# A vision tower whose instruction orders come from a planner: other durations in the planner, token requests as a queue of their own, and another written order for TensorE

## The chip, the core and the metric

The kernel runs on one core of a Trainium2 chip. A core has a matrix engine (TensorE, PE in the profile; its weight loads stand apart as PEld), three engines for element-wise work (VectorE or DVE, ScalarE or ACT, GpSimd or POOL) and SyncE (SP), which here issues DMA requests. Each engine takes its own instructions in their order and waits on semaphores for the others. The metric is the device time of one execution in microseconds (us); lower is better.

## What is computed

One tokenizer and one transformer layer over 16 images of 3 x 512 x 512, each cut into 1,024 patches of 16 x 16, with 256 features and 8 heads of 32. All in float32:

```python
h = patches(x) @ tok_W.T + tok_b                      # 16 x 1024 x 256
a = layernorm(h)
q, k, v = split(a @ w_qkv)                            # 8 heads of 32
k = sum(kan_a[f] * sin((f + 1) * k) + kan_b[f] * cos((f + 1) * k) for f in range(256))
h = h + softmax(q @ k.T * 32**-0.5) @ v @ w_out + b_out
a = layernorm(h)
shared = mlp(a, sW1, sW2, sW3)                        # 256 -> 256 -> 128 -> 256, relu
gate = softmax(a @ gW)                                # 4 experts, the best two kept
h = h + shared + sum(softmax(best two of gate) * expert(a))   # 256 -> 128 -> 64 -> 256
```

The sums over 256 frequencies for each of the keys' 16 x 1024 x 256 elements are the heavy part outside the matrix products.

## The kernel before

**The pieces.** An image's keys are worked through in 32 *groups* of 8 rows. A group needs three wave tiles of 128 x 1024. The two slow ones (`w`) are loaded by DMA, broadcast from the keys' angles in DRAM (`ud`, `load_waves`). The fast one (`f`) is spread by VectorE's shuffle from a tile `src` (`load_source`, `spread_waves`). GpSimd multiplies each tile by its lane's integer frequency (`turn_waves`, `L1026`), ScalarE takes its sine (`sine`, `L1036`). Then TensorE mixes the two slow tiles with the coefficients (`mix`, `L1056`, output `kan`), VectorE multiplies by the fast one (`times_fast`, `L1070`), and TensorE adds the products of two groups up (`add_up`, `L1089`, output `red`). Eight groups make the keys of a pair of heads; they go through DRAM (`kd`) into `k4`. An *attention* (half the queries of one pair, 8 an image, 128 in all) has 8 scores (`score`, `L1155`, output `sT`), 8 exponentials (`exponential`, `L1170`, `es`) and 8 weighings of the values (`weigh`, `L1188`, `av`), followed on VectorE by a reciprocal, two products and a check (`normalize`).

**Rounds.** Four groups and one attention make a round. ScalarE's big work has a fixed order: a round's twelve sines (six for each two groups), a load of the exponential's table, and eight exponentials of the attention two rounds behind; the next round's first sine loads the sine's table again.

**The chains.** All the rest (tokens, layernorms, keys, queries, values, projection, gates, networks) is written as Python generators on four chains, which `yield` the engine that they need and a duration. `tokens` is on chain 3, with first layernorms; keys, queries and values on chain 0; projection, gates and networks on chain 1. Their TensorE pieces share two PSUM banks, `side0` and `side1`. `kan` and `sT` tiles share two others in turn, so each waits until the tile two before it has been used up: a `kan` by `L1070`, an `sT` by its exponential.

**The planner.** `run` goes through a written order, `ORDER`: one character for each of TensorE's 3,840 pieces (M mix, R add_up, S score, W weigh, a digit for the next piece of that chain). Before each it lets the other engines do whatever they can start up to TensorE's own time (`others`), each the step that can start first by the planner's clocks. Each step has a cost and the steps that it depends on (`put`), and when a step is laid, its instructions are recorded on its engine in that order. On the chip only the orders remain, with semaphores between them: the clocks decide the order on VectorE, ScalarE's chain work, GpSimd and SyncE, and nothing else.

`ORDER` has a head of 664 pieces, a block of 240 pieces (one image's worth) eleven times, and a tail of 536.

**Tilings.** `mix` uses the array as 64 x 32 tiles, `av`, `red`, `gate` and the experts' second layer as 128 x 32, scores and transposes whole. A chain piece of the kind `ANY` takes the tiling that the array is in, by `tiling_of`; as 128 x 32 it issues four narrow matmuls (`L322`) for each whole one (`L319`). `retile` puts a cost on a change of tiling.

**Token requests.** There are three `x` buffers. `tokens` multiplies a chunk of 128 patches, calls `load_x` for the chunk three ahead, which waits for the same buffer, and then has VectorE add the bias:

```python
            del chunks[b, j]
            load_x(b, j + XBUFS)
            for action in deferred.pop(j + b * (N // XT), ()):
                action()
            yield DVE, 0.41
            nc.vector.tensor_add(h[:, t, :], ps, tokb)
```

`transfer` keeps SyncE's clock and that of the DMA engines; `sent` is the same for a store that a chain makes.

Of the kernel before, what the change touches and what calls it, by code (L numbers as in the profile page):

```python
# [22 lines left out]
N = 1024  # L23
# [20 lines left out]
XT = 128  # L44
# [13 lines left out]
LAG, LANDS, TABLE, PER_COLUMN = 0.06, 2.0, 1.28, 1.0 / 600  # L58
SWITCH = {None: 0.21, (128, 32): 0.13, (64, 32): 0.13}
# [6 lines left out]
    "333333313131300003000030M0M000MMR3R3M3M",  # L66
    "303RMM3MR330M3R3M03MSSRSSWSSWSSWWWW0MWM",
    "WMMRSSSRSWSSWSSW0WWWWMMW3MMRSSRSSWSSWSSW0WW0MMWWWMMRSSRSSWSSWSSW0WWMWWMWMRMSSSWSSWSSWSRW"
    "WWWWMMMMRSSSWSSWSSWSRWWWWW0M0MM0RMS0SSWSSWSWSWSWWW3W3MR13M3MMRSSRSSWSS1SSWWWW3WMWWM3RMS1"
    "SS1SS0SSWWWMS3WR3WWWWM0MMRMS0SS1SR1SSWW1S1SW0W1WW1MMW1W1MM1SSRWSS0SS1WSSWW10RWMWWW1MM10M"  # L70
    "S1SSRWSWR1SS1WSS1W1MMWWMMWW0SS1R1SS1WW1SS1SSW1WRW1WMMW3WMMRS1SS1SW1SS3SSW1WR1WWWWWMM13MM"
    "1RSS0SS0SS0SWWWSWWWR3MMW1WS10S1RSS1S3MMWSS3WRWWSW1WWMW31MM0SS1SSRMS1SSWWWSWR3WWWW3MM131M"
    "S1RSSWWMWSSR3S1S3S1WWW01M1WW1MM0RSS1SWSSWMS1SSWRWW01MW1WWMM101SSRMW1SSWWSS1RSS101MMWWWWW"
    "MS3SSWRMWSS1S01SSW1RW0W3MMWWRWSS131SS1MMWWSS1SSRWWW1WWW101",
    (
        "MM10RMM1SS01SS1SS1WWSS1WWWRWWWMM10MMRS3S1SS1SSWWWSS3RWWWW1W3MM0RMM3SSRSWWWSS1SS1S3WWWMMW"
        "3W311MSRM1WS1S3SWWS3S1SSRW1W0WMM1WWRMM10SS1SS1WW1SS0SSWWRW1WWW0MM10MM1SS1RRWWSS0S1SWSS1W"
        "WWWWMM1S0SRWSSWMMWS1S31SSWRW3WW1WMM3MMR1SS1SS1SSWWWSS1WRWW1WW101"
    )
    * 11,  # L80
    "MM1MM1SSRRWWS1S0SS0SSWWW130MMWW1WRM1MS1",
    "3SSRWWWSS31SS1SW1WWWWMM3RM1S0SSWSS1SSWWMSWR3WWM3WWMM13S1SR1MSWWRS3S1SWS3SWWW01MM1WW10MMR"
    "1SS1SSRWSS1S1WWS0WWWWWMM101MM1SS1RS1SRSSWWWSS01WWMMWWWMS1SSWSSRW0SS1S1WMWWR1WWMM10W1MMR1"
    "SS1SSWWSS1SSWWWR1WM1WW101MM10S1MR1SSWRS1SWSSWS1WWMMWWWRMM1SS0SSWWSSWSSRWWW1WW1M0M1RSS1SS"
    "WSSWSMWSM1WWRWM1W1WMM1RM1SS1SSWWSS1SSWR1W1W1W1MM1WWR1SM1SS1SSWWSSWS1MWWRWMWWM1SS1SWSMSRM"
    "WS1SS1WR1WWW1WW1MM1M1RSS1SWWSS1SSWSWMWW1RW1MM1RW1MM1SSR1SSWWSS1WWSSWWWW1SSSWSSWWSSWSSWWW"
    "W1SS1SS1SWWSSWWWWWW11110110111110000101000100101001000100",
# [3 lines left out]
def plain_path(ctx: ExitStack, tc: tile.TileContext, a: dict, out: bass.AP, verdict: bass.AP):  # L91
# [185 lines left out]
    locks = set()  # L277

# [10 lines left out]
    def retile(tiling):  # L289

        same = now["tiling"] == tiling
        now["tiling"] = tiling
        return 0.0 if same else SWITCH[tiling]

# [35 lines left out]
    def transfer(took, issue=0.0, ready=0.0):  # L330

        clock[SP] = max(clock[SP], ready) + issue
        now["dma"] = max(now["dma"], clock[SP]) + took
        return now["dma"] + LANDS

    def sent(took, issue):

        return transfer(took, issue, chains[now["chain"]]["ready"])
# [9 lines left out]
    def step(c):  # L348

        ch = chains[c]  # L350
        now["chain"] = c
        bank, ch["bank"] = ch["bank"], None
        need = ch["need"]
        before = now["stream"]
        on = need[0] if isinstance(need, tuple) and need[0] in clock else None
        if on == PE:
            now["piece"] = tiling_of(need[2])
        if on:
            at = max(clock[on], ch["ready"] + LAG)
            if on == PE:  # L360
                at = max(at, banks(c)[0][0] + LAG)
            ch["ready"] = clock[on] = at + (need[1] or 0.0)
            if bank is not None:
                free[bank] = ch["ready"]
        elif isinstance(need, tuple):
            ch["ready"] = max(ch["ready"], done[need])
        while True:
            if ch["gen"] is None:
                if not ch["gens"]:
                    ch["need"] = None  # L370
                    break
                ch["gen"] = ch["gens"].pop(0)
            try:
                ch["need"] = next(ch["gen"])
                break
            except StopIteration:
                ch["gen"] = None
        if on == PE:
            took = PER_COLUMN * (now["stream"] - before) + retile(now["piece"])
            now["piece"] = None  # L380
            ch["ready"] = clock[PE] = at + took
# [31 lines left out]
    def lay(engine, queue):  # L413
# [3 lines left out]
        done[key] = clock[engine]  # L417
# [37 lines left out]
    def lay_fixed(kind):  # L455

        cost, deps, key, action = queues[PE][kind][0]
        user = USERS.get(kind)
        at = begin(PE, deps + (bigs[-2:-1] if user else []))

        def lay_it():
            queues[PE][kind].pop(0)
            clock[PE] = done[key] = at + cost + retile(TILINGS.get(KINDS[kind]))
            if user:
                bigs.append((user, *key[1:]))
            action()

        return at, lay_it
# [27 lines left out]
    def load_x(b, j):  # L496

        b, j = b + j // (N // XT), j % (N // XT)
        if b < B:
# [5 lines left out]
            done["x", b, j] = transfer(1.75, 0.6, clock[PE])  # L505
# [38 lines left out]
    def tokens(b, half):  # L544
# [5 lines left out]
        for t in range(4):  # L550
# [13 lines left out]
            load_x(b, j + XBUFS)  # L564
            for action in deferred.pop(j + b * (N // XT), ()):
                action()
            yield DVE, 0.41
            nc.vector.tensor_add(h[:, t, :], ps, tokb)  # L568
# [94 lines left out]
    def values(b):  # L663
# [5 lines left out]
        for t0 in range(0, NT, 2):  # L669
# [11 lines left out]
            yield ACT, 0.62  # L681
# [142 lines left out]
    def networks(b, half, late=False):  # L824
# [25 lines left out]
        def first_of_expert(e):  # L850
            yield ANY
            ps = hidden(lambda c: w1e[:, 2 * e + c, :], "e1p")
            yield ACT, 0.6
# [4 lines left out]
        def second_of_experts(u, e1):  # L858
# [11 lines left out]
            yield ACT, 0.6  # L870
# [15 lines left out]
        for m in range(2):  # L886
            yield ANY
            ps = hidden(lambda c, m=m: w1s[:, c, ts(m, P)], "s1p")
            yield ACT, 0.6
# [14 lines left out]
        yield ACT, 0.6  # L904
# [42 lines left out]
        done["written", b, half] = sent(1.6, 0.5)  # L947
# [13 lines left out]

    def load_waves(g, j):


        def action():
# [6 lines left out]
            done["loaded", g, j] = transfer(1.9)  # L972
# [3 lines left out]
        put(SP, "waves", 1.1, deps, ("load", g, j), action)  # L976

    def load_source(p):


        def part(j, blk):
            def action():
# [11 lines left out]
                landed = transfer(0.4)  # L994
# [7 lines left out]
        for j in range(2):  # L1002
            for blk in range(2):
                put(SP, "source", 1.4, deps, ("part", p, j, blk), part(j, blk))

    def spread_waves(g):
# [11 lines left out]
        put(DVE, "spread", 1.28, deps, ("spread", g), action)  # L1018

    def turn_waves(g, j):  # L1020
# [8 lines left out]
        put(POOL, "turn", 1.87, [dep], ("turn", g, j), action)  # L1029

    def sine(g, j, change):
# [8 lines left out]
        put(ACT, "fixed", 0.96 + change, [("turn", g, j)], ("sine", g, j), action)  # L1040
# [26 lines left out]
    def times_fast(g):  # L1067
# [4 lines left out]
        put(DVE, "prod", 1.16, [("mix", g), ("sine", g, 2)], ("prod", g), action)  # L1072
# [29 lines left out]
    def finish_keys(p):  # L1102


        def action():
# [3 lines left out]
            done["kd", p] = transfer(1.4, 1.1, done["keys", p])  # L1109
# [4 lines left out]
    def stack_keys(p, half):  # L1114

        def action():
# [3 lines left out]
            done["stacked", p, half] = transfer(1.9)  # L1120

        deps = [("kd", p)] + ([("score", 2 * p - 1, 4 * half + 3)] if p > 0 else [])
        put(SP, "keys", 0.8, deps, ("k4", p, half), action)
# [3 lines left out]
    def stack_queries(att):  # L1127
# [3 lines left out]
        def action():  # L1131
# [8 lines left out]
            done["q4", att] = transfer(1.6)  # L1140

        deps = [("queries", b, i // 2)] + ([("score", att - 2, NT - 1)] if att > 1 else [])
        put(SP, "queries", 2.0, deps, ("q", att), action)
# [6 lines left out]
    def score(att, kc):  # L1150
# [13 lines left out]
        put(PE, "S", 0.47, deps, ("score", att, kc), action)  # L1164

    def exponential(att, kc):
# [9 lines left out]
        put(ACT, "fixed", 0.99, deps, ("exp", att, kc), action)  # L1176
# [28 lines left out]
    def normalize(att):  # L1205
# [8 lines left out]
        def divide(half):  # L1214
# [11 lines left out]
            put(DVE, "norm", 0.4, deps, ("divide", att, half), action)  # L1226
# [15 lines left out]
        put(DVE, "norm", 1.67, [("av", att, NT - 1)], ("reciprocal", att), reciprocal)  # L1242
        for half in range(2):
            divide(half)
        put(DVE, "norm", 0.4, [("divide", att, 1)], ("norm", att), check)
# [30 lines left out]
    for g in range(total):  # L1276
# [6 lines left out]
        times_fast(g)  # L1283
    for p in range(total // 8):
# [7 lines left out]
    for rd in range(B * RI + 2):  # L1292
# [15 lines left out]
        put(ACT, "fixed", TABLE + 0.2, [], ("table", rd), table)  # L1308
# [752 lines left out]
```

## Time and profile before

| | us |
|---|---|
| median of 3 runs (3911.86 to 3915.78) | 3914.31 |
| the profiled execution | 3913.84 |
| its span, first to last instruction | 3912.3 |
| TensorE's mean granted clock | 0.994 of full |

The longest groups (busy time, mean duration in ns, idle time of the engine just before them and what ended most of it):

```profile
L1026 POOL TENSOR_TENSOR w<-w,lane 128x1024 int32<-128x1024 int32 x1024 | 1925.6, 1897 | 391.6 <-DMA w<-ud 273.0
L1170 ACT ACTIVATE es<-sT 128x1024 f32<-128x1024 f32 x1024 | 1014.9, 1022 | 340.9 <-PE sT L1155 296.8
L1036 ACT ACTIVATE w<-w 128x1024 f32<-128x1024 int32 x1024 | 1013.3, 1046 | 70.5 <-POOL w L1026 67.3
...
L1155 PE MATMUL sT<-q,k 128*128 128x512 f32 x2048 | 708.1, 455 | 22.0 <-ACT es L1170 12.3
L1011 DVE STREAM_SHUFFLE f<-src 128x1024 int32<-128x1024 int32 x512 | 683.1, 1373 | 0.4
L1188 PE MATMUL av<-es,v 128*32 128x256 f32 x8192 | 638.7, 383 | 14.8 <-ACT es L1170 12.3
```

A matmul of float32 operands stands in the trace as two records, one of the scores' and of `wb` as one; overlapping records of TensorE are normal, since matmuls are pipelined and a record's end is modelled.

### The profile page before, as it was taken

The numbers are of one execution on the slowest core, as the hardware profiler recorded it, in microseconds if no ns is written. First come the engines' busy times: TensorE is split into PE (matmuls) and PEld (weight loads), VectorE is DVE, ScalarE is ACT, GpSimd is POOL, SyncE is SP. The second block draws the span as 40 slices with busy tenths as digits, with TensorE's granted clock in tenths as the row PEclk, the third lists the DMA queues.
The fourth block names the chain that finished last, engine by engine and source line by source line (L and its number), as shares of the span: only waits on it lengthen the run. The fifth ranks groups of instructions, "written<-read, shape, count | busy, mean of one in ns | idle before, by whom it ended". The sixth has DMA issues, their size and how long they took to land.

```text
span 3912.3 us, 102935 instructions
## 1 busy us (share of the span) xinstructions
PE 3811.7 (97%) x40337; PEld 1949.1 (50%) x40337; DVE 2525.4 (65%) x4075; ACT 3264.3 (83%) x3939; POOL 3197.1 (82%) x2328
## 2 busy tenths in 40 slices
PE   7899999999999999999999999999999999999998
PEld 4334454554545555455454545545455554544444
DVE  4756757666675766757667575766767667576552
ACT  2788888888888888888888888888888888888983
POOL 3988879788788878879788788878879888888870
PEclk9999999999999999999999999999999999999999
DMA  7997968888788888878888788787878888778760
GB/s 231 283 255 213 278 197 248 256 230 259 214 260 231 233 262 228 259 218 257 243 236 260 211 255 249 225 255 222 267 214 252 258 226 265 223 231 254 213 179 21
DMA packets 589665, 916.53 MB, mean 234 GB/s; under 512 B 60877, under 2 KB 179573, under 8 KB 589173
## 3 DMA queue, kind: packets, MB, share of 16 engines
q1 hardware_dynamic: 588036, 909.40, 80.0%
q8 instruction: 321, 5.26, 0.6%
q14 instruction: 172, 1.40, 0.1%
q10 hardware_dynamic: 1136, 0.47, 0.0%
HBM read 758.64 MB, written 150.99 MB: 233 GB/s over the span
## 4 chain that ended last, share of the span: by engine, by line
PE 70%; ACT 9%; DMA 9%; POOL 4%; DVE 3%; issue 3%; SPq 1%; ACTq 0%; POOLq 0%; DVEq 0%
PE av L1188 17%; PE sT L1155 10%; PE kan L1056 9%; DMA w<-ud 6%; PE red L1089 4%; PE tok L319 4%; ACT w L1036 3%; PE e1p L319 3%; PE e3p L319 3%; PE tok L322 3%; POOL w L1026 2%; ACT f L1036 2%; PE e1p L322 2%; ACT es L1170 2%; PE s1p L319 2%
## 5 line engine op out<-in xcount | busy, mean ns | idle before, releaser
L1026 POOL TENSOR_TENSOR w<-w,lane 128x1024 int32<-128x1024 int32 x1024 | 1925.6, 1897 | 391.6 <-DMA w<-ud 273.0
L1170 ACT ACTIVATE es<-sT 128x1024 f32<-128x1024 f32 x1024 | 1014.9, 1022 | 340.9 <-PE sT L1155 296.8
L1036 ACT ACTIVATE w<-w 128x1024 f32<-128x1024 int32 x1024 | 1013.3, 1046 | 70.5 <-POOL w L1026 67.3
L1026 POOL TENSOR_TENSOR f<-f,lane 128x1024 int32<-128x1024 int32 x512 | 971.4, 1897 | 105.2 <-DVE f L1011 89.8
L1070 DVE TENSOR_TENSOR f<-kan,f 128x1024 f32<-128x1024 f32 x512 | 605.0, 1214 | 207.9 <-ACT f L1036 112.1
L1155 PE MATMUL sT<-q,k 128*128 128x512 f32 x2048 | 708.1, 455 | 22.0 <-ACT es L1170 12.3
L1011 DVE STREAM_SHUFFLE f<-src 128x1024 int32<-128x1024 int32 x512 | 683.1, 1373 | 0.4
L1188 PE MATMUL av<-es,v 128*32 128x256 f32 x8192 | 638.7, 383 | 14.8 <-ACT es L1170 12.3
L1188 PE MATMUL av<-es,ones 128*32 128x256 f32 x8192 | 631.0, 380 | 0.0
L1056 PE MATMUL kan<-w,coef 64*32 64x512 f32 x8192 | 542.3, 599 | 20.5 <-ACT w L1036 13.2
L1036 ACT ACTIVATE f<-f 128x1024 f32<-128x1024 int32 x512 | 518.9, 1045 | 4.2 <-POOL f L1026 4.2
L1155 PEld LDWEIGHTS sT<-q,k 128*128 128x128 f32 x2048 | 350.8, 189 | 316.8 <-issue 137.1
L1188 PEld LDWEIGHTS av<-es,v 128*32 128x32 f32 x8192 | 234.7, 109 | 356.2 <-issue 232.9
L1188 PEld LDWEIGHTS av<-es,ones 128*32 128x32 f32 x8192 | 267.1, 110 | 176.4 <-issue 1.4
L1212 DVE RECIPROCAL rc<-av 128x256 f32<-128x256 f32 x128 | 224.7, 1755 | 164.4 <-PE av L1188 164.3
L1056 PEld LDWEIGHTS kan<-w,coef 64*32 64x32 f32 x8192 | 129.3, 105 | 317.2 <-issue 127.3
L1089 PE MATMUL red<-f,pack 128*32 128x512 f32 x2048 | 271.6, 603 | 0.0
L319 PE MATMUL tok<-wt,x 128*128 128x256 f32 x768 | 182.6, 390 | 18.8 <-DMA x<-in_xT 11.1
L531 ACT ACTIVATE hn<-h,less,rstd 128x256 f32<-128x256 f32 x256 | 140.7, 591 | 52.4 <-POOL less L523 51.8
L1036 ACT ACT_TABLE_LOAD x128 | 164.2, 1283 | 17.8 <-DMA w<-ud 15.5
L322 PE MATMUL tok<-wt,x 128*32 128x256 f32 x3072 | 178.0, 380 | 1.0 <-DVE h L568 1.0
L319 PEld LDWEIGHTS tok<-wt,x 128*128 128x128 f32 x768 | 148.1, 195 | 54.9 <-issue 21.3
(148 smaller groups left out, 4264.5 us busy)
## 6 DMA issues: line engine op xcount, KB each, us to landing
w<-ud SPq DMA_DIRECT2D x2048, 256.0 KB
q<-qd SPq DMA_DIRECT2D x512, 128.0 KB
k<-kd SPq DMA_DIRECT2D x256, 256.0 KB
x<-in_xT SPq DMA_DIRECT2D x128, 384.0 KB
ud<-u SPq DMA_DIRECT2D x64, 512.0 KB
ud<-ui SPq DMA_DIRECT2D x64, 512.0 KB
src<-ud SPq DMA_DIRECT2D x512, 64.0 KB
qd<-qhi SPq DMA_DIRECT2D x64, 256.0 KB
```

Source lines behind the costliest of these rows:

```text
L319: nc.tensor.matmul(out=out, lhsT=lhsT, rhs=rhs, start=start, stop=stop)
L322: nc.tensor.matmul(out=out[ts(i, 32)], lhsT=lhsT[:, ts(i, 32)], rhs=rhs, start=start, stop=stop)
L1011: nc.vector.stream_shuffle(w, sources[g // 8].rearrange("p r n -> p (r n)"), [4 * (g % 8) + i // 8 for i in range(32)],)
L1026: nc.gpsimd.tensor_tensor(w, w, f.to_broadcast([P, N]), ALU.mult)
L1036: nc.scalar.activation(x, w, AF.Sin, scale=TURN * 2.0**-32)
L1056: nc.tensor.matmul(out=ps[ds(64 * j + 32 * blk, 32), ts(r, 512)], lhsT=coef[ts(r, 64)].rearrange("p e f j -> p (e f j)"), rhs=w[ts(r, 64), ...
L1070: nc.vector.tensor_mul(w, kan.pop(g), w)
L1089: nc.tensor.matmul(out=rows_of_pair[p][ts(2 * i + r, 32), :], lhsT=pack[:, ds(PACK0 - 16 * (k % 2) - 2 * (k // 2), 32)], rhs=prod[:, ts(r, ...
L1155: nc.tensor.matmul(out=ps[:, ts(s, 512)], lhsT=k4[kc // 4][:, s, ts(kc % 4, P)], rhs=q4[:, s, :], start=True, stop=True,)
L1170: nc.scalar.activation(es, scores.pop(kc), AF.Exp, scale=SCALE)
L1188: nc.tensor.matmul(out=acc[0][ts(i, HD), ts(half, 256)], lhsT=ones32 if half else v[:, kc, p % NPAIR, ts(i % 2, HD)], rhs=es[:, ds(512 * ( ...
L1212: nc.vector.reciprocal(rc[0], acc[0][:, 256:512])
```

## The change

It has four parts.

1. *Durations.* The costs of the planner's steps and its constants take other values. A step's engine is free after its cost, and its result is there a `TAIL` later, by engine. A score after another tiling costs `RELOAD` more; a whole-array piece that had to wait costs `STALL`.
2. *Requests.* `transfer` gives each DMA its own issue time and lets one start only when the eighth before it has landed (`lanes`). Stores that a chain makes count as there `WRITTEN` earlier.
3. *Token requests.* `load_x` is no longer called in `tokens`. `load_tokens` puts each request into a queue of its own on SyncE, `tokens`, which depends on the end of the token piece that uses the buffer. `tokens` marks that end, after a `yield` that lets the piece's end be known; the deferred loads of weights now come after the bias's addition.
4. *Order.* `ORDER` is another string with the same counts of each character, and the same lengths of head, block and tail.

```diff
-LAG, LANDS, TABLE, PER_COLUMN = 0.06, 2.0, 1.28, 1.0 / 600
-SWITCH = {None: 0.21, (128, 32): 0.13, (64, 32): 0.13}
+WRITTEN = 0.9
+LAG, LANDS, TABLE, PER_COLUMN, STALL = 0.07, 2.3, 1.29, 1.0 / 600, 0.15
+RELOAD = 0.07
+TAIL = {"pe": 0.27, "act": 0.08, "dve": 0.06, "pool": 0.0, "sp": 0.0}
+SWITCH = {None: 0.14, (128, 32): 0.12, (64, 32): 0.12}
...
-    "333333313131300003000030M0M000MMR3R3M3M",
+    "33333331311003033003000M0M00M0M0MRR330M",
...
     (
-        "MM10RMM1SS01SS1SS1WWSS1WWWRWWWMM10MMRS3S1SS1SSWWWSS3RWWWW1W3MM0RMM3SSRSWWWSS1SS1S3WWWMMW"
-        "3W311MSRM1WS1S3SWWS3S1SSRW1W0WMM1WWRMM10SS1SS1WW1SS0SSWWRW1WWW0MM10MM1SS1RRWWSS0S1SWSS1W"
-        "WWWWMM1S0SRWSSWMMWS1S31SSWRW3WW1WMM3MMR1SS1SS1SSWWWSS1WRWW1WW101"
+        "MM1MM1RSS10SS1SSW1WW1SSW0RWWWWMM1RMM3SS0SSWWWSS1SS3RWW1WWW3MM10MM3SRRWSS1SSWS1SSWW3WWWMM"
+        "3W31S1RM1MWS13SSR3SS1SSWW0WWW1WMMW1RMM1S0SS1SSW1SS0SWWWR1WWWW01MM10MM1SSR1WSSRWW1SS0SS1W"
+        "WWWWMM1S0SRWSSWWMMW1SS3SS1WWWR13WMM31MM1RSS1SSWWWSS1SSRWWW1WW101"
     )
     * 11,
...
-    def transfer(took, issue=0.0, ready=0.0):
-
-        clock[SP] = max(clock[SP], ready) + issue
-        now["dma"] = max(now["dma"], clock[SP]) + took
+    def transfer(took, issue=0.0, ready=0.0, parts=2):
+
+        clock[SP] = max(clock[SP], ready)
+        for _ in range(parts):
+            clock[SP] = max(clock[SP], lanes[0] + LAG) + issue / parts
+            now["dma"] = max(now["dma"], clock[SP]) + took / parts
+            lanes[:] = [*lanes[1:], now["dma"] + LANDS]
         return now["dma"] + LANDS
...
-            done["x", b, j] = transfer(1.75, 0.6, clock[PE])
+            done["x", b, j] = transfer(1.7, 0.4, parts=1)
...
             del chunks[b, j]
-            load_x(b, j + XBUFS)
+            held = chains[now["chain"]]["bank"]
+            yield lambda: True
+            chains[now["chain"]]["bank"] = held
+            mark("token", b, j)
+            yield DVE, 0.34
+            nc.vector.tensor_add(h[:, t, :], ps, tokb)
             for action in deferred.pop(j + b * (N // XT), ()):
                 action()
-            yield DVE, 0.41
-            nc.vector.tensor_add(h[:, t, :], ps, tokb)
...
+    def load_tokens(i):
+        def action():
+            load_x(0, i + XBUFS)
+
+        put(SP, "tokens", 0.0, [("token", *divmod(i, N // XT))], ("tokens", i), action)
...
-        put(SP, "waves", 1.1, deps, ("load", g, j), action)
+        put(SP, "waves", 0.0, deps, ("load", g, j), action)
...
-        put(ACT, "fixed", 0.96 + change, [("turn", g, j)], ("sine", g, j), action)
+        put(ACT, "fixed", 0.946 + change, [("turn", g, j)], ("sine", g, j), action)
...
-        put(ACT, "fixed", 0.99, deps, ("exp", att, kc), action)
+        put(ACT, "fixed", 0.91, deps, ("exp", att, kc), action)
...
+    for i in range(B * N // XT - XBUFS):
+        load_tokens(i)
```

In what follows `kan` 111, say, is group 111's mix; `sT` 25.0 and `av` 25.0 are the first score and the first weighing of attention 25 (counted over all images); `lnT2`, `q6` and so on are the third transpose, the seventh query piece of the run.

## The prediction

> **What bounds the kernel now.** I read the busy lines first, then the chain that ended last, then who TensorE waited for, then the wait list and busy times by stage.
>
> ```profile
> span 3912.3 us, 102935 instructions
> PE 3811.7 (97%) x40337; PEld 1949.1 (50%) x40337; DVE 2525.4 (65%) x4075; ACT 3264.3 (83%) x3939; POOL 3197.1 (82%) x2328
> ...
> PE 70%; ACT 9%; DMA 9%; POOL 4%; DVE 3%; issue 3%; SPq 1%; ACTq 0%; POOLq 0%; DVEq 0%
> ```
>
> TensorE sets the end: 97% busy, 70% of the chain. Its busy time counts modelled ends and a wait in mid-piece, so it can't tell how much of that is work. The start and modelled end of every matmul can. I cut the matmuls into the 3,841 pieces of the written order and took as the time of a piece the end of its last matmul less that of the piece before. The kinds are sharp: `av` takes 0.863 us (median of 728) after a piece of its own tiling and 1.001 after a full-array one; `kan` 0.859 and 1.019; `sT` 0.467 and 0.661. The tenth percentile of each kind (by tile, tiling and the tiling before it) is its cost with nothing to wait for. Over the order these sum to 3,706 us. The pieces took 3,889; the first starts at 11.1 and its end comes at 15.4; after the last one 7.9 us are left. So **waits, with slow clock, are 183 us**: 46 in the first 78 pieces (to 172 us), 50 in the next 586 (to 772), 61 in the eleven repeats of the 240-piece block (772 to 3369: 236.1 an image, of which 230.6 are work), 26 in the tail. No order of these pieces can save more than this 183.
>
> Who is late, in the eleven repeats (columns: us in total, times, longest):
>
> ```profile
> PE av L1188 <- ACT es L1170: 12.3, 11, 1.9
> PE sT L1155 <- ACT es L1170: 5.1, 12, 0.7
> PE kan L1056 <- DVE f L1070: 3.6, 11, 0.3
> ```
>
> and in the start, by stage (busy us of PE, PEld, DVE, ACT, POOL, then TensorE's granted clock, DMA share, GB/s):
>
> ```profile
> 40.00:80.00 40.00, 27.61 (x68) 15.43 (x67) 23.64 (x39) 6.56 (x9) 14.72 (x10) 0.79 0.69 233
> 80.00:120.00 40.00, 34.71 (x283) 15.47 (x285) 29.88 (x39) 26.29 (x40) 38.30 (x26) 0.87 0.93 268
> 120.00:172.00 52.00, 45.55 (x492) 17.99 (x484) 35.60 (x56) 38.29 (x43) 51.33 (x33) 0.97 0.92 280
> ```
>
> In the repeats ScalarE is late in short stretches; at the start nothing is busy until 75 us, and then GpSimd is full (38.3 of 40, 51.3 of 52).
>
> **The change part by part.**
>
> *Instruction counts.* VectorE, ScalarE, GpSimd and SyncE issue the same instructions in another order. TensorE has 3,841 pieces as before; a few `tok`, `k`, `q`, `proj`, `s1p`, `e1p` pieces take the other tiling at the same streaming time.
>
> *Tiling changes.* Counted in the built order, these go from 1,259 to 1,297: +1 in the first 78 pieces, +13 in the next 586, +1 a block, +13 in the last 537. With each piece at its cost above, after's order sums to 3,711: **+4.8 us** (+2.2 to 772 us, 0 in the block, where cheaper kinds of change make up for the extra one, +1.9 in the tail, rest rounding). The Trainium skill speaks against the change here: TensorEngine Tiling (Array Packing), Key Properties, has a change of tiling mode drain the array, and TensorE: Matmul & The Clock Gate, Single matmul latency, gives a lone warm matmul 398 cycles beyond its columns, 0.166 us. By that rule, an estimate: 38 × 0.166 = 6.3 us. The rows (0.138, 0.160, 0.194 by kind) decide: 4.8.
>
> *The eleven repeats.* The waits recur at the same places of each block; summed over nine places they are 4.2 of 5.5 us an image. Most end with ScalarE, between the last score of a round and the first work that needs the next round's waves or exponentials. In between ScalarE has two table loads (1.28) and twelve sines (about 0.95 each from start to start). So what counts is how much TensorE work stands between. By the piece costs, before against after: from `sT` 22.7 to `kan` 101, 8.3 to 8.9 (its second `kan` waited 0.42); 23.7 to `kan` 107, 14.6 to 15.4 (0.23); 24.7 to `kan` 109, 7.2 to 8.9 (0.25); 24.7 to `av` 25.0, 20.4 to 21.2 (0.27 and 0.50); 25.7 to `av` 26.0, 23.9 to 24.7; 26.7 to `av` 27.0, 21.9 to 22.8. `sT` 23.7, which waited 0.55 behind two scores in a row, gets an `e3p` piece (2.83) ahead of it. The wait of 0.30 at `sT` 29.1 gets `s1p` (1.85) ahead in place of `gateT`. But 27.7 to `av` 28.0 stays 16.7 us, piece for piece the same, so the largest wait (1.32; the 12.3 us row) stays; and 28.7 to `av` 29.0 shrinks, 23.2 to 22.1. Gone: 0.42 + 0.23 + 0.25 + 0.55 + 0.30 = 1.75, and about half of 0.27 + 0.50 + 0.43; new at round 28, about 0.3. That is 2.0 an image: **−22 us**.
>
> *A wait that is added.* `kan` 111 now comes second after `sT` 25.0, so it needs the bank that this score's exponential frees. Queued behind it stand every `av` and `sT` of the round. ScalarE's rows at this place of one image:
>
> ```profile
> 2050.06 0.58 ACT L540 COPY hT<-lnT 128x512 f32<-128x512 f32 x1
> 2050.65 1.28 ACT L1306 ACT_TABLE_LOAD   x1
> 2051.95 0.20 ACT L1306 ACTIVATE few<-few 128x1 f32<-128x1 f32 x1
> 2052.06 1.01 ACT L1170 ACTIVATE es<-sT 128x1024 f32<-128x1024 f32 x1
> ```
>
> The score started at 2050.23 and its exponential ended at 2053.07, 2.8 us later. In after's order `sT`, `lnT`, `red`, `kan` and `gate` (0.65 + 0.44 + 0.86 + 1.02 + 0.57 = 3.5 us) cover this. I cost it at 0; without that cover, at up to 3.6 us, the one such wait that the list has (`kan` on an exponential, at 375 us).
>
> *The start.* Group 0's fast waves hold up GpSimd:
>
> ```profile
> 63.22 4.66 SPq L990 DMA_DIRECT2D src<-ud  x6
> 67.99 0.38 SPq L623 DMA_DIRECT2D ud<-u  x1
> 68.48 0.41 SPq L623 DMA_DIRECT2D ud<-ui  x1
> 68.94 2.04 SPq L990 DMA_DIRECT2D src<-ud  x2
> ...
> 65.78 1.89 POOL L1026 TENSOR_TENSOR w<-w,lane 128x1024 int32<-128x1024 int32 x1 [1.82 <-DMA w<-ud]
> 75.50 1.90 POOL L1026 TENSOR_TENSOR f<-f,lane 128x1024 int32<-128x1024 int32 x1 [7.82 <-DVE f L1011]
> ```
>
> The last two `src` requests stand behind `ud` of the fourth `k` piece, and VectorE has a `q` split ahead of the shuffle. In after the eight `src` requests follow the third `ud` in one run, and the first shuffle comes ahead of the first `q` split. VectorE's `k` chain ends about as before (62.6), so `src` is out about 5 us sooner and GpSimd, full from there to 172 us, starts its run about 5 us sooner. Against this: `lnT2` now follows `k0` directly at about 37 us and waits for the second half's `hn` (39.20 to 41.27), about 4 us where a `tok` piece stood. That piece is spent later, where `tok` and `q` waited 4.7, 4.8 and 7.5. I take **−5 us** for the first 78 pieces (bounds +3 and −15).
>
> *To 772 us and the tail.* Of the 50 us, `kan` and `sT` waits of 5.3, 3.7, 2.9, 2.6, 2.3 and 1.9 are a third; after's order puts fillers ahead of some (`q6` before `kan` 23; the block's pacing from 230 us on), but also has 51 `kan` pieces that need a bank from the newest scores, against 39. No row prices this: between 0 and −25, I take −11, nearest to the share by which the repeats fall. The tail is a dependent chain of networks in both: −3 (0 to −8).
>
> *Token requests.* Each `x` request was queued at the start of the `tok` piece whose buffer it needs, so SyncE stood for it: L501 waits for `tok` sum to 133 us (89.3 + 43.7). Now it is queued once the piece is over. Behind it stand mostly `w<-ud` requests, and GpSimd's waits for these (273 us) end seldom on TensorE's path in the repeats. I count it in the sums above, at nothing by itself. In the block the fourth `tok` of an image is asked for 24 pieces ahead, so a later request costs nothing; in the first 60 pieces it may.
>
> **Sum**, against the profiled execution's own 3,913.84 us (span 3,912.3; 0.5 us under the median of the runs): +4.8 − 22 − 5 − 11 − 3 = −36, so **3,878 us**.
>
> **The rivals.**
>
> *Waits only change places* (0.16). An order searched by a model fits the model's errors too, and ScalarE's stretches are as long as before: the 1.32 us wait is untouched. Then only the start's −5 and the switches' +4.8 are left: 3,914, between 3,900 and 3,920. Against it: the cover between rounds grows in five places.
>
> *Most waits go* (0.17). All nine places but the 1.32 (−2.9 × 11 = −32), a third of the start's 96 (−32), −8 in the tail, +4.8: 3,847. For it: GpSimd paces the start and is let go 5 us sooner, and with shorter gaps the clock comes back (0.79 and 0.87). Against it: ScalarE's twelve sines don't get shorter.
>
> *Slower: the bank behind the table load* (0.07). If ScalarE reaches `sT` 25.0 over 0.7 us later than before against TensorE, `kan` 111 stands, at up to 3.6 us an image, and the round's gains go with it: +40 + 4.8 − 5 − 11 − 3 = +26, 3,940. For it: that row of 3.6, and the 51 such pieces against 39. Against it: the cover of 3.5 us for a need of 2.8.
>
> The forecast's own case (0.60) spans 3,860 to 3,898. **Range 3,845 to 3,905**: it takes in most of the case below and a part of the one above. What this kernel's measurement can tell from no change is about 0.2%, 8 us. Faster: 0.60 + 0.17 + 0.05 of the second case = 0.82; same 0.08; slower 0.07 + 0.03 = 0.10.
>
> **What would show it.** The repeats at about 234 us an image; `av` on `es` still about 12 us over eleven times; `sT` on `es` and `kan` on `f` near nothing there; no `kan` on `es` row of some 10 us or more (else the slower case); GpSimd's first `f` at about 70 us in place of 75.50 and the granted clock from 40 to 120 us above 0.83; TensorE's tiling costs as now. I am wrong if the repeats stay at 236, or if the start loses what they gain.

## The result, and the profile after

The changed kernel takes **3,895.78 us** (median of 5 runs, 3,889.19 to 3,898.54), the kernel before 3,911.86 us (5 runs beside it). The ratio is 0.9954, with a 95% interval of 0.9942 to 0.9966: 16 us faster, where 36 were forecast. The profiled execution took 3,898.54 us, against 3,913.84 before.

The head of the page of the changed kernel (span; busy time of each engine; share of each engine in the chain that ended last):

```profile
span 3896.9 us, 103136 instructions
PE 3791.3 (97%) x40457; PEld 1942.1 (50%) x40457; DVE 2544.1 (65%) x4075; ACT 3256.0 (84%) x3939; POOL 3193.6 (82%) x2328
...
PE 77%; ACT 10%; DMA 7%; DVE 2%; issue 2%; POOL 1%; SPq 1%; ACTq 0%; POOLq 0%; DVEq 0%
```

TensorE's share of the chain has risen from 70% to 77%, and POOL's has fallen from 4% to 1%. Now the list of who TensorE waited for in the eleven repeats (767 to 3357 us), with total, times and longest wait in us:

```profile
PE av L1212 <- ACT es L1194: 11.1, 11, 1.0
PE gate L816 <- ACT hT L555: 9.5, 11, 1.2
PE kan L1080 <- ACT es L1194: 5.5, 11, 0.5
```

The `av` row is still there (12.3 before). The `sT` row (5.1) is gone from the top. Two rows are new: `gate` on ScalarE's copy `hT`, and `kan` on `es`. Third, the start by stage (busy us of PE, PEld, DVE, ACT, POOL, then TensorE's granted clock, DMA share, GB/s):

```profile
40.00:80.00 40.00, 27.35 (x80) 16.33 (x80) 22.07 (x35) 7.33 (x10) 14.34 (x11) 0.85 0.63 205
80.00:120.00 40.00, 30.45 (x221) 11.05 (x224) 20.86 (x33) 24.19 (x38) 33.12 (x23) 0.85 0.91 278
120.00:172.00 52.00, 43.66 (x488) 17.51 (x483) 35.99 (x58) 32.33 (x37) 48.60 (x31) 0.93 0.93 266
```

From 80 us on GpSimd does less than before (33.12 against 38.30, then 48.60 against 51.33): the start has become slower. The cut into pieces (end of a piece's last matmul less that of the piece before) puts numbers on the stretches. "Wait" is the time above the pieces' own cost; "first 78 pieces" counts from the end of the very first piece.

| stretch | before: time, wait | after: time, wait | difference | forecast |
|---|---|---|---|---|
| first 78 pieces | 156.7, 45.7 | 166.0, 54.9 | +9.3 | -5 |
| next 586 | 601.4, 50.2 | 584.5, 31.3 | -16.9 | -11 |
| eleven repeats | 2596.9, 60.6 | 2589.8, 52.6 | -7.1 | -22 |
| tail | 534.0, 26.2 | 530.1, 20.5 | -3.9 | -3 |

These sum to -18.6. The first piece ends 1.1 us later, and the time after the last piece grows by 2.1, which gives the -15.4 of the spans. The pieces' own cost, summed by the same costs over the new order, is 3,711.0 against 3,706.2, as forecast; the common kinds cost the same in the changed kernel (medians of 0.863 and 1.001 for `av`, 0.858 and 1.019 for `kan`). The largest gain, 16.9 us, is in the stretch for which the forecast had no price, and the start lost more than the repeats gained.

### The profile page after: what moved, and what is told of

Read it like the earlier page. It is cut to its first block, busy times and chain, and to the rows that moved or that the text cites. A ratio compares the mean times of both kernels' runs of the same rounds, so it can differ in the third digit from the quotient of the medians.

```text
span 3896.9 us, 103136 instructions
## 1 busy us (share of the span) xinstructions
PE 3791.3 (97%) x40457; PEld 1942.1 (50%) x40457; DVE 2544.1 (65%) x4075; ACT 3256.0 (84%) x3939; POOL 3193.6 (82%) x2328
## 4 chain that ended last, share of the span: by engine, by line
PE 77%; ACT 10%; DMA 7%; DVE 2%; issue 2%; POOL 1%; SPq 1%; ACTq 0%; POOLq 0%; DVEq 0%
PE av L1212 19%; PE sT L1179 11%; PE kan L1080 9%; PE red L1113 5%; PE tok L325 4%; ACT w L1060 4%; DMA w<-ud 3%; PE e1p L325 3%; PE tok L328 3%; PE e3p L325 3%; PE e1p L328 2%; ACT f L1060 2%; PE k L325 2%; PE proj L325 2%; PE s1p L325 1%
## 5 line engine op out<-in xcount | busy, mean ns | idle before, releaser
L1194 ACT ACTIVATE es<-sT 128x1024 f32<-128x1024 f32 x1024 | 1004.0, 1023 | 369.0 <-PE sT L1179 305.9
L1179 PE MATMUL sT<-q,k 128*128 128x512 f32 x2048 | 689.1, 450 | 14.0 <-DVE f L1094 7.8
L1080 PE MATMUL kan<-w,coef 64*32 64x512 f32 x8192 | 529.3, 598 | 15.3 <-ACT w L1060 9.6
L1060 ACT ACTIVATE f<-f 128x1024 f32<-128x1024 int32 x512 | 514.2, 1046 | 13.1 <-POOL f L1050 13.1
L1179 PEld LDWEIGHTS sT<-q,k 128*128 128x128 f32 x2048 | 360.7, 189 | 254.0 <-issue 110.7
```

The source lines that it names most:

```text
L1060: nc.scalar.activation(x, w, AF.Sin, scale=TURN * 2.0**-32)
L1080: nc.tensor.matmul(out=ps[ds(64 * j + 32 * blk, 32), ts(r, 512)], lhsT=coef[ts(r, 64)].rearrange("p e f j -> p (e f j)"), rhs=w[ts(r, 64), ...
L1179: nc.tensor.matmul(out=ps[:, ts(s, 512)], lhsT=k4[kc // 4][:, s, ts(kc % 4, P)], rhs=q4[:, s, :], start=True, stop=True,)
L1194: nc.scalar.activation(es, scores.pop(kc), AF.Exp, scale=SCALE)
```

## The experiments

The change has three separable parts. **O** is TensorE's written order. **T** is the token requests as a queue of their own on SyncE. **D** is the rest of the planner: traced durations, engine tails and DMA lanes. Six runs take them singly and in pairs; the others edit the order in one, two or three places. All times in one table; the stretches are in us, from the profiled execution of each run:

| kernel | median us | ratio to before, 95% interval | first 78 | next 586 | repeats | tail |
|---|---|---|---|---|---|---|
| before | 3911.86 | 1 | 156.7 | 601.4 | 2596.9 | 534.0 |
| changed (O, T, D) | 3895.78 | 0.9954 (0.9942 to 0.9966) | 166.0 | 584.5 | 2589.8 | 530.1 |
| T | 3916.26 | 1.0015 (1.0009 to 1.0022) | 156.4 | 604.3 | 2590.3 | 536.1 |
| O | 3958.77 | 1.0123 (1.0107 to 1.0138) | 169.4 | 601.6 | 2620.3 | 542.4 |
| D | 4023.03 | 1.0282 (1.0269 to 1.0296) | 175.0 | 606.2 | 2677.8 | 542.1 |
| T, D | 3934.43 | 1.0057 (1.0043 to 1.0071) | 173.1 | 597.6 | 2595.3 | 537.9 |
| O, T | 3918.57 | 1.0017 (1.0011 to 1.0023) | 167.8 | 600.6 | 2587.5 | 537.7 |
| O, D | 3944.73 | 1.0095 (1.0081 to 1.0109) | 173.4 | 592.8 | 2620.6 | 531.2 |
| changed + round 25 | 3889.57 | 0.9945 (0.9932 to 0.9959) | 165.0 | 583.2 | 2585.5 | 529.6 |
| changed + tok 8 | 3887.12 | 0.9947 (0.9933 to 0.9960) | 162.1 | 581.5 | 2586.5 | 529.4 |
| changed + red 0, 1 | 3891.03 | 0.9953 (0.9942 to 0.9965) | 167.6 | 580.4 | 2588.6 | 529.4 |
| changed + all three | 3888.70 | 0.9945 (0.9932 to 0.9957) | 166.4 | 581.1 | 2584.5 | 532.4 |
| changed + round 25, tok 8 | 3884.07 | 0.9936 (0.9923 to 0.9950) | 160.6 | 583.2 | 2582.8 | 529.6 |
| the same + wb 9 | 3886.60 | 0.9934 (0.9921 to 0.9947) | 161.8 | 583.6 | 2582.5 | 531.3 |

The kernel before, run beside each group of these, took 3,908.9 to 3,911.9; between rows the ratios are to be compared. The stretches are of one execution each, so a single us in them is not much.

### The planner with the old order (T, D)

The changed kernel with the `ORDER` of before:

```diff
-    "33333331311003033003000M0M00M0M0MRR330M",
+    "333333313131300003000030M0M000MMR3R3M3M",
...
```

> The change's planner (traced durations, lanes, token queue) with TensorE's order of before. Theory A (the time is carried by TensorE's literal order: which operation covers a round's handovers): as before, 3,912 +-5 us, recurring waits of an image still near 5.5 us, 1,259 tiling changes. Theory B (the gain is carried by the new orders of the other engines and of SyncE): near the changed kernel, about 3,897, with the recurring waits of an image near 4.8 us although TensorE's order is the old one. A worse result than before (over 3,918) would say that the new clocks fit only the order that was searched with them.

It is 0.57% slower than before: neither theory held, and the third case of the expectation came, clocks that fit only the order they came with. The repeats' waits are 5.4 us an image, near the 5.5 of before, as A said. The loss is in the first 78 pieces, +16.4 us. There `lnT` 4 and `lnT` 6 wait 13.9 and 13.1 us for ScalarE's `hn` (a layernorm's result; `rstd` and `less` are its scale and shift, made on GpSimd). Before, the four `hn` for `lnT` 4 ran in one piece at 98.30. Rows of ScalarE in this kernel (start, duration, operation, idle before and its releaser):

```profile
104.48 1.58 ACT L546 ACTIVATE hn<-h,less,rstd 128x256 f32<-128x256 f32 x3 [0.97 <-POOL less L538]
106.33 1.06 ACT L1060 ACTIVATE w<-w 128x1024 f32<-128x1024 int32 x1 [0.27 <-POOL w L1050]
107.29 0.59 ACT L546 ACTIVATE hn<-h,less,rstd 128x256 f32<-128x256 f32 x1
```

The fourth `hn` stands behind one more sine, and the first three wait for GpSimd's `less`, which the new clocks placed behind turns of the waves. This happens although GpSimd's first `f` starts at 70.52, the 5 us sooner of the forecast. Releasing GpSimd sooner at the start is therefore not enough for a shorter start.

### The order with the old planner (O)

The kernel of before with the `ORDER` of the change:

```diff
-    "333333313131300003000030M0M000MMR3R3M3M",
+    "33333331311003033003000M0M00M0M0MRR330M",
...
```

> The planner of before (old durations, token requests within x's queue) with TensorE's order of the change. Theory A (order carries it): as the changed kernel, 3,896 +-5, first 78 pieces about 166 us, gate4c's wait of 1.1 us in each repeat there. Theory B (planner and token queue carry it): as before, about 3,912, or worse, since SyncE's and the other engines' orders are then placed by clocks that do not fit.

Theory A fell and B's "or worse" came: 1.2% slower. In the repeats the waits are 7.6 us an image, and the list names them:

```profile
PE kan L1056 <- ACT es L1170: 12.2, 11, 1.1
PE av L1188 <- ACT es L1170: 11.1, 11, 1.0
PE kan L1056 <- ACT w L1036: 8.8, 15, 0.8
```

The first row is the mechanism of the forecast's slower rival: `kan` 111 stands behind the bank of `sT` 25.0, 1.18 us in each image. The third is new: `kan` 99 waits 1.94 us an image for a sine. (By the pieces this is 21 us; the list counts only the idle time between records, 8.8.)

### Token queue alone (T), and taken out of the change (O, D)

T puts this into the kernel before, and O, D takes the same out of the changed one. With it go, in O, D and in O, T, the deferred weight loads to the other side of the bias's addition, and in O, D the request's ready time in the planner; these were not separated.

```diff
-            load_x(b, j + XBUFS)
+            held = chains[now["chain"]]["bank"]
+            yield lambda: True
+            chains[now["chain"]]["bank"] = held
+            mark("token", b, j)
...
+    for i in range(B * N // XT - XBUFS):
+        load_tokens(i)
```

> The kernel of before with one part of the change: token requests are a queue of their own on SyncE, old durations, old order of TensorE. Theory A (a request in time is enough, SyncE is not on the path): 3,912 +-3 us, SyncE's 133 us of waits for tok go to other waits. Theory B (the requests that stood behind waits for tok held up SyncE's other transfers): several us faster, 3,900 to 3,908, with less idle time of GpSimd ended by the copies of ud into w.

> The changed kernel with one part undone: the token requests are issued within the tok piece again, after its matmuls are queued, as before, and SyncE waits for them; durations and TensorE's order stay the change's. Theory A (the request's place counts for nothing by itself): within 4 us of the changed kernel, SyncE waits some 130 us for tok again. Theory B (SyncE's queue is what the new order was searched with, so other transfers and then GpSimd's turns come late where the order leaves no cover): slower by 8 to 25 us, most of it in the first 664 pieces. Planner and order apart were slower than before, by 23 and 47 us, so a part of the planner must carry that; this run asks whether it is this part.

Alone the queue brings nothing: 0.15% slower over 21 runs that spread from 3,910.6 to 3,923.5 (the profiled one has shorter repeats and a longer rest). Taken out of the changed kernel it costs 49 us by the medians (3,944.73 against 3,895.78) and 55 by the ratios (1.0095 and 0.9954). That is theory B, and more than B's 25. B's place was wrong, however: 31 of it lie in the repeats, not in the first 664 pieces (15.7). There `kan` 99 waits 2.66 us an image, against 0.39 in the changed kernel. SyncE's waits for `tok`, first without the queue:

```profile
SPq L516 <- PE tok L328: 130.5, 50, 8.7
...
SPq L516 <- PE tok L325: 92.4, 45, 11.7
```

and with it, in the changed kernel:

```profile
SPq L516 <- PE tok L328: 25.9, 15, 5.3
...
SPq L516 <- PE tok L325: 20.9, 17, 5.6
```

SyncE stands 223 us where it stood 47. The timeline of one image shows who pays. Without the queue (this image's block starts at 1734.9), rows of SyncE, then GpSimd, then ScalarE:

```profile
1704.00 2.84 SPq L1011 DMA_DIRECT2D src<-ud  x4
1709.01 0.40 SPq L516 DMA_DIRECT2D x<-in_xT  x1
1709.45 2.73 SPq L1011 DMA_DIRECT2D src<-ud  x4
1712.28 10.63 SPq L992 DMA_DIRECT2D w<-ud  x16
...
1717.14 1.89 POOL L1047 TENSOR_TENSOR w<-w,lane 128x1024 int32<-128x1024 int32 x1 [7.76 <-PE sT L1176]
...
1738.48 1.06 ACT L1057 ACTIVATE w<-w 128x1024 f32<-128x1024 int32 x1 [1.71 <-POOL w L1047]
1740.33 1.06 ACT L1057 ACTIVATE w<-w 128x1024 f32<-128x1024 int32 x1 [0.80 <-POOL w L1047]
```

and with it (block starts at 1706.7):

```profile
1674.94 5.56 SPq L1014 DMA_DIRECT2D src<-ud  x8
1680.61 11.38 SPq L995 DMA_DIRECT2D w<-ud  x16
1692.39 1.31 SPq L516 DMA_DIRECT2D x<-in_xT  x2
...
1685.41 1.90 POOL L1050 TENSOR_TENSOR w<-w,lane 128x1024 int32<-128x1024 int32 x1 [4.26 <-DMA w<-ud]
...
1707.51 2.95 ACT L1060 ACTIVATE w<-w 128x1024 f32<-128x1024 int32 x3
```

Without the queue one `x` request stands between the two halves of `src` and another ahead of them. SyncE issues nothing from 1706.84 to 1709.01, and the sixteen `w` requests begin 22.6 us ahead of the block's start instead of 26.1. GpSimd's first turn follows its first `w` request by 4.9 us here and by 4.8 there, so it comes 17.8 ahead instead of 21.3 (the `sT` that its row names as releaser is only the last event that the profile saw, not shown to be what it waited for). ScalarE idles 1.71 and 0.80 us where its three sines ran in one piece, and `kan` 99 waits 2.79 in this image, 2.66 on average. With the queue two `x` requests come behind the sixteen `w`.

### Order and queue without the durations (O, T), and the durations alone (D)

> TensorE's order of the change and the token queue, with the durations and lanes of before. Theory A (the token queue is the part of the planner that the new order needs; the traced durations are detail): near the changed kernel, 3,896 +-8, kan 99 of the repeats waits under 0.5 us. Theory B (the durations are needed as much): the 49 us that the token queue was worth are about halved, 3,915 to 3,940, and what stays late is work of ScalarE and VectorE in the first 664 pieces, not kan 99.

> The kernel of before with the new durations and lanes alone: token requests within the tok piece, TensorE's order of before. If the loss of 23 us of the whole planner with the old order comes from its durations (norms of the second image placed behind GpSimd's and ScalarE's waves in the start): about 3,930, first 78 pieces near 173 us. If it comes from durations and token queue together: about 3,912.

O, T is 0.17% slower than before. Its repeats are as short as the changed kernel's (2,587.5, `kan` 99 at 0.50). What it lacks are 16 us in the next 586 pieces and 8 in the tail: theory B in the total. As it says, `kan` 99 is not what stays late, but a third of the loss lies in the tail, and which engine comes late was not traced. D alone is the worst of all, and neither figure foresaw that. Its repeats lose 81 us, 7.4 an image; 3.07 of that are `gateT` on ScalarE's `rows` (the gate's outputs), 1.87 `e2p` on ScalarE's `last` (a copy of values). Why these two come so late was not traced further. With the queue added to D (T, D) they are gone, and the repeats are back at 2,595.3.

So the eight combinations say: **no part and no pair gains; only the three together do.** This is said of these two orders and these two planners, and of no others. What the queue is worth depends on the rest: by the ratios it costs 0.15% alone, and gives 1.1% with O, 2.2% with D and 1.4% with both. With the new order it is worth some 32 us of the repeats whatever the durations (2,620 to 2,588 and 2,590); the durations are worth some 24 to 26 in the rest of the kernel, once order and queue are in place.

### The added wait at round 25

```diff
-        "3W31S1RM1MWS13SSR3SS1SSWW0WWW1WMMW1RMM1S0SS1SSW1SS0SWWWR1WWWW01MM10MM1SSR1WSSRWW1SS0SS1W"
+        "3W311MSRM1WS13SSR3SS1SSWW0WWW1WMMW1RMM1S0SS1SSW1SS0SWWWR1WWWW01MM10MM1SSR1WSSRWW1SS0SS1W"
```

> The changed kernel with the repeated block's local sequence of before at round 25 of attention: lnT 26, lnT 27, kan 110, sT 25.0, red 54, kan 111, gate4c. Theory A (moving sT 25.0 ahead of lnT 27 and kan 110 made lnT 27's copy fall behind ScalarE's sine and gate4c wait 1.07 us in each image): gate4c and kan 111 together go from 1.64 back to about 0.77 us an image, eleven repeats 2,589.8 to about 2,580, the total about 3,886. Rival (ScalarE's own row of work sets the pace of that round whatever TensorE's order): the wait turns up at another operation of the same round, total 3,896 +-3.

At the site theory A is right to the hundredth: `gate` 4c (the `gate` piece of that round) and `kan` 111 go from 1.07 + 0.57 to 0.00 + 0.50, with 0.27 at `lnT` 27 (0.77 in all, as before the change). Rows of TensorE in one image of the changed kernel:

```profile
2037.33 0.43 PE L816 MATMUL gate<-hT,gw 128*32 128x128 f32 x8
2038.97 0.43 PE L816 MATMUL gate<-hT,gw 128*32 128x128 f32 x8 [1.21 <-ACT hT L555]
2039.90 1.09 PE L1080 MATMUL kan<-w,coef 64*32 64x512 f32 x16 [0.50 <-ACT es L1194]
```

and ScalarE beside it:

```profile
2036.95 1.28 ACT L1332 ACT_TABLE_LOAD   x1
...
2038.35 0.57 ACT L555 COPY hT<-lnT 128x512 f32<-128x512 f32 x1
2038.82 1.03 ACT L1194 ACTIVATE es<-sT 128x1024 f32<-128x1024 f32 x1
```

The copy that `gate` needs and the exponential that `kan` needs both stand behind the table load. With the old sequence the copy is still behind it (2035.23, load at 2033.83), but `kan` runs ahead of `gate`, which starts at 2036.95 without a wait. So the edit left the copy behind the load, and theory A is wrong on what put it there. Not TensorE's order did, but the durations: with those of before (before, T, O and O, T) the copy starts some 0.6 us ahead of the load in all eleven images, and with the new ones (T, D; D; O, D; the changed kernel and this one) 1.40 behind it. In O and in O, T, where the copy comes first, `gate` does not wait; there `kan` 111 waits 1.18 us for the exponential. The total follows only in part: repeats -4.3 us of the -9.6, since `kan` 115 now waits 0.39 us, where it had not. By the ratios the whole is 0.9945 against 0.9954, which is within their intervals; the waits show the effect, the times alone do not.

### Three edits at the start, singly and together

```diff
-    "33333331311003033003000M0M00M0M0MRR330M",
+    "33333331311300033003000M0M00M0M0MRR330M",
```

(tok 8 ahead of `lnT` 2), and

```diff
-    "33333331311003033003000M0M00M0M0MRR330M",
+    "33333331311003033003000M0M00M0M0RRM330M",
```

(red 0 and 1 ahead of `kan` 4). A third kernel has both, and the edit at round 25.

> The changed kernel with the ninth tok piece put back between k 0 and lnT 2. Theory A (the first 78 pieces lost time because lnT 2 stood there and waited about 3 us with nothing to cover it, and the clock fell): lnT 2's wait falls from 4.5 to about 1 us, the fourth k piece and all that hangs on it come about 3 us sooner, first 78 pieces 166 to about 162, total 3 to 4 us under the changed kernel. Rival (GpSimd, full from 75 us on, sets the start's end): lnT 2's wait goes, but piece 664 ends within 1 us of where it did (767 us) and the total stays.

> The changed kernel with red 0 and red 1 ahead of kan 4 again. Theory A (red 0 and red 1 behind kan 4 made VectorE's shuffles and with them GpSimd's turns late, so k 4 waited 5.3 us behind hnT's copy): red 0 about 6 us sooner than 105 us, GpSimd's idle time of 2.9 us at 108 gone, k 4's wait under 2 us, first 78 pieces 166 to about 161, total 4 to 5 us under the changed kernel. Rival: kan 4's wait of 5.9 us only moves to the pieces behind it, first 78 pieces unchanged within 1.5 us.

> The changed kernel with three local edits of TensorE's order together: the repeated block's old sequence at round 25, tok 8 back between k 0 and lnT 2, red 0 and red 1 ahead of kan 4. If the losses are local and add: 3,889.6 (the first edit alone) less 3 less 4, about 3,882, first 78 pieces near 157. If the start is set by GpSimd or by how the planner lays the other engines round each order: no better than the first edit alone, 3,890, or worse.

*Tok 8*: theory A in the start, at the size expected (`lnT` 2 waits 1.7 us in all, by the pieces, instead of 4.5). TensorE's rows in the changed kernel:

```profile
41.20 1.95 PE L334 MATMUL lnT<-ident,hn 128*128 128x128 f32 x4 [2.95 <-ACT hn L546]
43.83 1.12 PE L334 MATMUL lnT<-ident,hn 128*128 128x128 f32 x4 [0.68 <-ACT hnT L555]
44.73 4.20 PE L325 MATMUL tok<-wt,x 128*128 128x256 f32 x12
```

and with tok 8 put back:

```profile
35.96 1.98 PE L325 MATMUL k<-hnT,wk 128*128 128x512 f32 x4
37.78 2.75 PE L325 MATMUL tok<-wt,x 128*128 128x256 f32 x12
41.34 0.87 PE L334 MATMUL lnT<-ident,hn 128*128 128x128 f32 x3 [0.81 <-ACT hn L546]
```

The same twelve matmuls take 2.75 us in the second and 4.20 in the first. GpSimd's first `f` starts at 71.60 instead of 75.53, and the first 78 pieces take 162.1. It is not caught up later: piece 664 ends 7 us sooner (760.1 against 767.1). By the ratios the total is 2.7 us less, which is within the intervals. What stands behind stays as it was: `kan` 4, `k` 4 and `lnT` 6 wait 5.89, 5.33 and 3.87 us in both kernels.

*Red 0, 1*: the rival, nearly (1.5 us was its bound). GpSimd's idle time of 2.86 us ahead of `f` goes and `kan` 4 waits 3.3 instead of 5.9, but `lnT` 4 then waits 9.7 us and the stretch is 1.6 longer. GpSimd in the changed kernel:

```profile
103.10 0.23 POOL L534 TENSOR_SCALAR rstd<-mv 128x4 f32<-128x4 f32 x1
...
107.90 1.89 POOL L1050 TENSOR_TENSOR f<-f,lane 128x1024 int32<-128x1024 int32 x1 [2.86 <-DVE f L1035]
```

and with the edit:

```profile
102.00 1.90 POOL L1050 TENSOR_TENSOR f<-f,lane 128x1024 int32<-128x1024 int32 x1
...
107.68 0.23 POOL L534 TENSOR_SCALAR rstd<-mv 128x4 f32<-128x4 f32 x1
```

As the waves came sooner, the planner put them ahead of the norm's `rstd`, which now comes 4.6 us later than in the changed kernel, and with it `hn`, `lnT` 4 and `k` 4. *All three*: no better than round 25 alone, the second case of its expectation; it contains the edit that loses.

### Two edits together, and one more

> The changed kernel with two local edits together: the old sequence at round 25 and tok 8 back between k 0 and lnT 2. Local and additive: first 78 pieces 162, repeats 2,585, total 3,896 less 6 less 7, about 3,882. If the planner lays the start anew: no better than 3,888.

> The run before, and in the repeated block wb 9 between sT 27.5 and sT 27.6 in place of q 18, which goes behind sT 27.7, so that ScalarE gets the last exponentials of round 27 about 1.2 us sooner and all up to the exponential of round 28 with them. If av 28.0 waits for ScalarE's chain from there (two exponentials, table load, twelve sines, table load, exponential): its wait of 1.22 us falls to 0.3 or less, for about 0.35 us more at sT 27.6 and 27.7, eleven repeats some 7 us shorter, total about 3,875. If the sines wait for GpSimd's turns instead: the wait stays at 1.2 and the total loses 3 to 4 us.

Round 25 with tok 8 adds up as expected: first 78 pieces 160.6, repeats 2,582.8, **3,884.07 us, ratio 0.9936 (0.9923 to 0.9950)**. By its ratio it is 25 us faster than the kernel before and about 7 us faster than the changed kernel, though the two intervals still overlap.

The further edit exchanges two pieces of the block so that ScalarE starts round 28 sooner:

```diff
-        "3W311MSRM1WS13SSR3SS1SSWW0WWW1WMMW1RMM1S0SS1SSW1SS0SWWWR1WWWW01MM10MM1SSR1WSSRWW1SS0SS1W"
+        "3W311MSRM1WS13SSR3SS1SSWW0WWW1WMMW1RMM1S0SS1SSW1SS0SWWWR1WWWW01MM10MM1SSR1WSSRWWSS1SS01W"
```

`av` 28.0 no longer waits, and yet nothing is gained. The first of TensorE's waits in its repeats:

```profile
PE sT L1179 <- ACT es L1194: 7.3, 22, 0.5
```

The row of `av` on `es` is gone, and a row of `sT` on `es` has come. By the pieces `sT` 27.6 and 27.7 wait 0.75 and 0.45 us in every image: the 1.22 us have moved. So `av` 28.0 did wait for ScalarE, as the first case of the expectation says, but starting ScalarE sooner cost as much as it gave. The expectation had 0.35 for these two; the repeats are 2,582.5 against 2,582.8.

## Why the prediction was right, and where not

**Right, and in part by luck.** Faster, and within the range. Five waits of the repeats that were to go are gone (0.42, 0.56, 0.23, 0.25 and 0.30 us at `kan` 101, `sT` 23.7, `kan` 107, `kan` 109 and `sT` 29.1), as the cover counted for each said; none was tried alone. `av` 28.0 stayed (1.22 of 1.32), as its unchanged 16.7 us of cover said. Tiling costs rose by 4.8 us, and the tail gave 3.9 us where 3 were forecast.

The total, however, came right by a term that was a guess. The prediction calls itself wrong "if the start loses what they gain", and that happened: the start lost 9.3 us, the repeats gained 7.1. What makes the kernel faster are the 16.9 us of the middle stretch ("No row prices this", taken as 11). The six waits that the prediction names there (5.3 down to 1.9, 18.7 in all) are 2.9 in the changed kernel. But they are also no more than 3.5 to 5.8 in O, in T, D, in O, T and in O, D, and there the stretch is 0.2 us longer to 8.6 shorter, since other waits took their place. Why so few others come when the three parts are together stays open.

**The wait that was added: mis-sized.** "I cost it at 0", with a cover of 3.5 us for a need of 2.8, and "about half of 0.27 + 0.50 + 0.43" gone. In its place the two pieces wait 1.64 us an image where `lnT` 27 and `kan` 111 had waited 0.77. The working took ScalarE's rows of the kernel before as they stood, with the copy `hT` ahead of the table load. The new durations put this copy behind the load (1.40 us after the load's start, where it had come 0.6 ahead of it), so `gate`, counted as cover, waited itself. And the cover was short without that too: with the new order and the old durations `kan` 111 alone waits 1.18 us. Against the forecast this is 0.87 + 0.38 = 1.25 us an image, which is nearly the size of the difference between the 2.0 forecast and the 0.72 measured (5.50 to 4.78). It is not the only term that was off: `kan` 99, `lnT` 24 and `sT` 24.0 wait 0.85 us more than before, unforeseen, and the 0.3 expected at round 28 and some small waits are missing. And putting the old sequence back returned 4.3 us of the repeats, not the whole.

**The start: wrong sign.** -5 forecast, +9.3 measured, and two steps failed. The first is "VectorE's `k` chain ends about as before (62.6)": it ended at 67.7. `lnT` 2 did wait, 2.95 us in the row above, and the granted clock then was 0.50 from 40.8 to 47.6, where the kernel before had 1.00. So `k` 1 started 4.0 us later (48.77 against 44.75; 1.4 us of that were there at the end of `lnT` 1). `k` 2, now behind `tok` 9 and `tok` 10, ended at 58.59 instead of 48.43. The `src` run, which did come in one piece as forecast, therefore began at 65.14, and GpSimd's first `f` stayed at 75.53. With tok 8 put back it came at 71.60. (The clock was not lower over the start as a whole: its mean from 40 to 172 us is 0.88 in both kernels.)

The second, and the larger, is "GpSimd, full from there to 172 us". The first 31 of the 78 pieces, the same ones in both orders, took 81.6 us where they had taken 80.4; the other 47 took 84.4 instead of 76.2. In these GpSimd is not full: 81.7 us of work from 80 to 172, where it had done 89.6. Rows of TensorE and GpSimd in the changed kernel:

```profile
101.67 3.48 PE L1080 MATMUL kan<-w,coef 64*32 64x512 f32 x16 [3.43 <-ACT w L1060]
113.26 2.07 PE L325 MATMUL k<-hnT,wk 128*128 128x512 f32 x2 [3.61 <-ACT hnT L555]
...
102.27 0.74 POOL L714 COPY v<-last 128x256 f32<-128x256 f32 x2 [2.55 <-ACT last L706]
```

By the pieces `kan` 4, `k` 4 and `lnT` 6 wait 5.9, 5.3 and 3.9 us, where they had waited 1.3, 0.0 and 0.1. Putting tok 8 back left these 84.4 us as they were, and moving red 0 and 1 moved the waits to `lnT` 4. The old order under the new planner also shows that an earlier first `f` does not make a shorter start: it comes at 70.52 there, and the start takes 173.1. What would take these waits away stays open.

**Token requests: "at nothing by itself" was wrong.** Out of the changed kernel they cost 49 us. The forecast read that GpSimd's waits for `w<-ud` end seldom on TensorE's path. That was true of the old order with the old durations, and there the queue indeed gives nothing. With the new durations in the old order it takes 89 us off (4,023.03 to 3,934.43). The new order puts `kan` 99 where the last sine has just come in the changed kernel (0.39 us of wait an image); without the queue SyncE's requests come late and it waits 2.66.

**The rivals.** "Waits only change places" is true at single sites (round 25 and round 28 show it), not of the whole. "The bank behind the table load" happens: `kan` 111 waits for this exponential 1.18 us an image when the order runs without the new durations, and 0.57 with them; "up to 3.6" never came.

## What to carry to other kernels

A written order and the planner that lays the other engines round it are one solution here: a test of one alone says little of the pair. Expect a local edit of one to be answered by the other. When a move puts a consumer behind a long fixed instruction of another engine, list everything that this engine has queued behind it, the small copies too, as the new planner will lay it and not as the old one did, and count as cover only pieces that need none of them. What a queue's standing time costs depends on what relies on the requests behind it (here from nothing to 89 us); judge it in the order and with the planner that it is to run with. And when a forecast's total comes true, check its terms: here the one without a price carried it.

## What the runs showed of the hardware

In the changed kernel TensorE's granted clock was 0.50 from 40.8 to 47.6 us: it fell 2.6 us into the wait of `lnT` 2 (38.25 to 41.20), and twelve 128x256 matmuls took 4.20 us instead of 2.75. The Trainium skill, TensorE: Matmul & The Clock Gate, What's actually happening, puts the fall at an idle window of about 3.4 us. Here less was enough. With tok 8 put back the clock fell as well, to 0.50 from 43.7 to 47.1 us, after idle stretches of only 0.81, 0.13, 0.16 and 0.14 us, and four `k` matmuls took 3.47 us instead of 1.98. In the kernel before, idle stretches of 0.88 and 0.68 us at the same place left it at 1.00. So the length of one wait does not decide it alone; what does was not tried.
